# Cross-attention with layernorm on one core: masks turned into biases by ScalarE, and another order of all engines

## The chip, the cores and the metric

The kernel runs on one core of one Trainium2 chip. The metric is device time in microseconds (us), the median of several runs. Before the change it is 514.48 us (three runs: 514.18, 514.48, 514.49).

The core has five instruction streams that run side by side and meet at semaphores: TensorE (PE, with its weight loads as PEld), VectorE (DVE), ScalarE (ACT), GpSimd (POOL) and SyncE (SP, which here only issues DMAs). Each stream executes strictly in the order in which its instructions stand.

## The reference

Queries come from `x` (4 batches of 2048 rows, 512 wide), keys and values from a context of 77 rows per batch; 16 heads of 32. A mask hides keys. The residual `x` is added and each row is layer-normalised with a gain and a shift.

```python
qs  = (q @ wq).reshape(Bq, Lq, H, HD).transpose(0, 2, 1, 3)
ks_ = (k @ wk).reshape(Bq, Lk, H, HD).transpose(0, 2, 1, 3)
vs  = (v @ wv).reshape(Bq, Lk, H, HD).transpose(0, 2, 1, 3)
scores = jnp.einsum('bhqd,bhkd->bhqk', qs, ks_) / jnp.sqrt(jnp.float32(HD))
scores = jnp.where(mask[:, None, :, :], -jnp.inf, scores)
attn_w = jax.nn.softmax(scores, axis=-1)
attn = jnp.einsum('bhqk,bhkd->bhqd', attn_w, vs)
attn = attn.transpose(0, 2, 1, 3).reshape(Bq, Lq, H * HD)
out = attn @ wo + q
mu = jnp.mean(out, axis=-1, keepdims=True)
var = jnp.mean((out - mu) ** 2, axis=-1, keepdims=True)
return (out - mu) / jnp.sqrt(var + EPS) * gamma + beta
```

The mask reaches the kernel as bytes, 96 per row (the last 19 of the 77 keys stand twice, for the two layouts of even and odd heads).

## The kernel before

The 8192 rows are 64 tiles of 128 rows, `t`. Two tiles are a block `b`, four a group `g` for the query projection, 16 a batch. The projections run in split single precision: an operand is a rounded part and a rest, and each product is three matmuls.

The work of a tile, by the letters that the kernel's order uses:

- `Q`: one quarter of a group's query projection, 12 matmuls of 512 columns; `q`: DVE copies it out of PSUM.
- `S t`: the scores of a tile on PE, into four PSUM banks, one for each head position. `T t.j`: DVE reads bank j, adds the mask's bias and takes the row maxima, four heads at a time. `e t.j`: ACT's exponentials, each with a read of its accumulator. `r`: DVE's reciprocal of the sums, `n`: POOL's product with it, `t`: DVE's transpose, `P`: DMAs that regroup the transposed weights.
- `V b`: the product with the values for a block, into two banks; `a` (ACT) and `b` (DVE) take the rounded part and the rest out of them. `O t`: the output projection, 12 matmuls. `+` or `&`: DVE adds the residual; `s`: DVE's moments; `v`, `k`, `f`, `)`: POOL's rsqrt, ACT's scale, POOL's gain and shift; `x` and `w` load and store rows. The last eight tiles take their end on DVE (`u`, `y`, `z`) and their residual rows from an `X` or `&`.
- `g`, `i`, `j`: the load of two of the four column chunks of a group's transposed `x`, its rounding on ACT and its rest on POOL.
- `L`: the load of a batch's mask, `M t.n`: DVE turns the bytes of n tiles into a bfloat16 bias (byte times -3.38e38). `= t.n`: the same on ACT.
- Before the steady state: `A`, `C`, `R`, `p` load the value and output weights, `F` and `G` take their rests on DVE (lines 355 and 367: two operands in SBUF), `B` projects the values, `D` takes them out, `Z` places them.

The order of all engines is written out by hand: the string `ORDER` holds some 2150 words, and each engine's instructions are issued in the order of its words. `SLOTS` says which buffer each allocation takes; the entry "mm" names one of the eight PSUM banks at each use. A PE step therefore waits for the words that empty its banks (`T`, `q`, `b`, `+`), for its operands, and for nothing else. Three buffers `pbuf` hold the score tiles in turn, and one buffer holds the mask bytes.

Of the kernel before, what the change touches and what calls it, by code (L numbers as in the profile page):

```python
# [33 lines left out]
for b in range(4):  # L34
# [19 lines left out]
e4.0 e4.3 r4 e6.3 e6.1 e6.0 q10 D1 P1.0s P1.4s Q8 q8 P1.5s T6.2 e6.2 P1.6s Q9 q9 P1.11s P1.9s P1.8s S5 T5.3 e5.3 T5.0
e5.0 n4 t4 S7 r6 T7.2 e7.2 T5.1 T7.3 e7.3 T7.1 P1.3s P1.10s T7.0 P1.7s e7.1 Z4.s Z5.s x2 g9 Q11 Q14 x3 T5.2 x0 q11 q14
n6 t6 e7.0 r7 Q13 q13 n7 S9 T9.0 T9.1 T9.2 e5.1 Z14.s Z16.s e5.2 r5 V1 a1.0 b1.0 t7 P3.5s e9.1 a1.1 b1.1 P3.3s P3.10s
V0 a0.0 T9.3 b0.0 P3.7s n5 P3.2s t5 P2.6s P3.8s P3.0s P3.9s a0.1 P3.1s i8 j8 i9 e9.0 e9.2 P3.11s N P3.6s O2 b0.1 +2 s2
P2.11s P3.4s Y0 P2.8s S8 T8.0 j9 O3 +3 T8.1 T8.2 s3 v1 O0 T8.3 S10 T10.3 T10.1 T10.2 P2.2s e9.3 r9 n9 e8.0 e8.1 e8.2
e8.3 r8 n8 +0 O1 +1 s1 P2.1s P2.5s t9 T10.0 k2 e10.1 P2.3s k3 f3 )3 P2.7s P2.0s e10.2 t8 Q15 e10.0 V3 a3.0 b3.0 S11
T11.2 a3.1 e10.3 T11.0 P2.9s r10 P2.10s P2.4s e11.2 g10 P4.7s P4.2s w3 s0 v0 Z7.s T11.1 e11.1 x4 P4.9s e11.0 Q12 q15  # L60
P4.4s q12 T11.3 b3.1 Q18 q18 S12 T12.3 P4.1s T12.0 M28.4 e11.3 r11 P4.5s x7 Z15.s V2 k1 T12.1 S13 n10 t10 e12.3 T12.2
n11 f2 t11 P4.10s g11 P4.6s e12.0 T13.1 T13.2 M16.4 P4.3s P4.11s T13.3 a2.0 P5.6s P4.0s e12.2 M20.4 P4.8s Z11.s P5.7s
x6 e12.1 a2.1 r12 n12 e13.2 O7 +7 P5.2s x5 P5.9s P5.4s i10 j10 T13.0 P5.11s )2 w2 b2.0 s7 P5.0s O6 Q17 q17 e13.1 S14
T14.1 T14.2 T14.0 e13.3 e13.0 k0 i11 e14.1 t12 r13 e14.2 T14.3 e14.3 Q19 q19 P5.8s Q16 +6 s6 b2.1 M24.4 f1 n13 S15
T15.2 t13 T15.1 V4 a4.0 P5.10s v3 k6 T15.0 f0 )0 )1 Z13.s Z12.s P5.1s x8 P5.5s g12 b4.0 q16 P6.5s w0 L2 e14.0 e15.0
j11 T15.3 a4.1 b4.1 f6 P5.3s O5 +5 O4 +4 S16 T16.3 T16.0 P6.9s r14 w1 n14 s5 T16.2 T16.1 P6.4s t14 P6.1s k7 f7 g13
e15.2 e15.3 e16.3 e15.1 r15 S17 T17.1 T17.3 T17.0 )6 n15 s4 v2 e16.2 Q21 q21 Q20 i12 )7 e16.1 O9 x9 T17.2 P6.10s P6.8s
e17.1 e17.0 i13 e16.0 j13 P6.0s P6.6s Z8.s P6.3s t15 +9 S18 T18.0 P6.2s T18.1 T18.2 T18.3 r16 n16 q20 V5 a5.1 O8 +8 s9
P6.7s P6.11s a5.0 e17.3 j12 e17.2 b5.1 P7.0s P7.7s r17 n17 Q23 s8 q23 V6 P7.6s e18.3 e18.0 e18.2 P7.8s x11 P7.3s g14
P7.2s P7.11s Z6.s t16 v4 e18.1 S19 T19.0 T19.3 e19.3 w7 P7.1s P7.5s T19.2 P7.9s r18 b5.0 P7.4s w6 t17 P8.4s n18 P7.10s  # L70
a6.0 g15 k4 e19.0 k9 f9 a6.1 P8.9s Q22 P8.3s P8.8s T19.1 q22 O11 +11 )9 i14 b6.0 b6.1 j14 e19.1 Q25 q25 S20 T20.0
T20.1 T20.3 x13 k8 k5 e19.2 P8.11s e20.3 x10 P8.1s g16 f4 )4 w4 t18 S21 T21.3 r19 w9 T21.1 f8 n19 P8.6s P8.2s f5 Q26
s11 q26 e20.0 T21.2 e21.2 e20.1 T20.2 e20.2 O13 +13 O10 P8.0s t19 P8.5s T21.0 r20 n20 +10 s10 S22 T22.1 T22.3 e21.1
i15 j15 P8.10s V7 a7.1 b7.1 e21.0 x12 P8.7s Q24 T22.2 P9.11s P9.7s a7.0 P9.3s )5 e21.3 e22.1 e22.3 s13 t20 Z9.s Z10.s
P9.10s P9.4s v5 k10 T22.0 e22.0 r21 n21 P9.0s O12 +12 b7.0 q24 s12 v6 k11 f10 f11 Q27 q27 S23 T23.1 T23.0 T23.2 V8 g17
)10 P9.8s P9.2s x16 w5 P9.5s x15 P9.9s e22.2 r22 t21 e23.0 k13 P9.1s n22 )8 S24 T24.1 T24.2 O15 +15 a8.0 b8.0 T24.0
T24.3 P9.6s a8.1 T23.3 P10.0s P10.7s O14 Q29 t22 e23.1 i16 e23.3 S25 b8.1 P10.10s P10.8s x14 T25.1 T25.0 w10 x17 w8
e23.2 e24.0 +14 q29 e24.2 s14 e24.3 j16 f13 )13 g18 i17 V9 a9.1 r23 n23 T25.2 T25.3 e25.0 e24.1 s15 v7 a9.0 k12 )11
j17 e25.1 e25.2 e25.3 O16 +16 s16 t23 r24 O17 P10.9s +17 S26 P10.5s P10.11s x18 P10.4s s17 T26.2 v8 b9.0 n24 P10.3s
P10.6s P10.1s T26.3 T26.0 b9.1 r25 n25 k17 P10.2s Q31 q31 P11.3s w13 P11.0s P11.7s g19 P11.1s P11.5s T26.1 Q30 q30 t24  # L80
Q28 q28 e26.2 S27 T27.3 T27.1 k16 e26.1 P11.8s f16 )16 x19 P11.9s T27.0 P11.11s P11.6s P11.10s P11.4s V10 t25 P12.10s
k14 f14 e27.1 S28 T28.1 T28.2 P11.2s a10.0 b10.0 T28.3 w11 P12.7s a10.1 f17 )17 w17 P12.8s P12.6s P12.3s e26.3 P12.11s
e26.0 r26 n26 k15 e27.3 f15 T27.2 e27.2 T28.0 e28.0 b10.1 i18 P12.0s x21 x20 Q33 q33 O19 P12.5s +19 t26 e27.0 e28.1
e28.2 s19 P12.2s O18 +18 S29 T29.1 T29.3 )14 V11 a11.1 f12 j18 e29.3 T29.2 e29.2 r27 n27 s18 T29.0 t27 w16 g21 P12.4s
S30 T30.1 b11.1 T30.3 O20 i19 v9 )15 P12.1s T30.2 +20 e28.3 r28 T30.0 s20 j19 k18 f18 a11.0 Q35 q35 Q32 w15 q32 b11.0
e29.0 P13.3s P13.6s e30.0 w14 P12.9s g20 x23 x22 P13.4s P13.2s n28 )18 P13.1s P13.5s P13.0s P13.7s e29.1 O21 +21 s21
M36.4 v10 M32.4 r29 n29 t28 Q37 S31 T31.0 T31.3 q37 P13.11s e30.2 w18 P13.8s e30.1 e30.3 k19 P13.10s V12 a12.0 f19
P13.9s )19 )12 w12 t29 P14.11s r30 e31.3 Q34 q34 a12.1 k21 f21 k20 f20 P14.0s P14.6s e31.0 T31.1 e31.1 T31.2 e31.2 i21
b12.1 O22 +22 S32 T32.0 T32.1 T32.2 e32.0 b12.0 i20 e32.1 T32.3 e32.3 O23 +23 s23 n30 t30 P14.10s Q38 q38 r31 j21 S33
T33.1 T33.0 V13 a13.0 b13.0 e32.2 P14.4s P14.7s P14.9s x25 x24 P14.5s P14.2s )21 n31 P14.1s P14.8s x27 P14.3s T33.2  # L90
e33.2 M44.4 S34 s22 r32 T33.3 )20 w20 e33.3 t31 a13.1 T34.0 T34.2 g23 M40.4 b13.1 O24 O25 w19 +24 P15.8s e33.0 e33.1
r33 w21 n32 x26 P15.2s L3 P15.4s v11 k22 k23 f22 n33 e34.2 t32 +25 T34.1 f23 )23 j20 Q39 q39 T34.3 e34.3 Q36 s24 q36
S35 T35.0 T35.1 T35.2 T35.3 e34.1 e34.0 P15.10s P15.0s t33 x28 P15.9s V14 a14.0 P15.1s a14.1 e35.0 r34 n34 i23 e35.2
# [5 lines left out]
Q40 q40 S39 T39.2 T39.0 T39.1 i25 j25 e39.0 f26 P17.11s V16 a16.1 r38 n38 t37 T39.3 S40 b16.1 T40.1 e39.3 a16.0 b16.0
T40.2 P17.4s w27 e39.1 w24 P17.3s O30 O31 P17.9s +30 T40.0 e40.1 P18.7s T40.3 t38 e39.2 x32 e40.0 v14 k28 )25 V17  # L100
a17.0 r39 n39 g24 i24 j24 S41 T41.0 T41.1 s30 f28 P18.10s O32 Q44 P18.11s k29 f29 T41.3 e41.3 )29 a17.1 t39 T41.2 Q45
b17.1 +32 x31 +31 s31 e40.3 e40.2 P18.9s b17.0 P18.0s r40 P18.4s P18.1s P18.5s P18.3s P18.8s e41.2 x33 e41.0 e41.1 v15
S42 s32 T42.1 P19.0s P19.8s P19.4s P19.10s )28 T42.2 T42.3 n40 P18.6s r41 n41 )26 P19.7s P18.2s O33 +33 q45 q44 w25
# [671 lines left out]
```

## Time and profile before

One execution was profiled: 514.09 us, of which 512.3 us are the span from the first to the last instruction.

| engine | busy us | share of the span |
|---|---|---|
| PE | 500.2 | 98% |
| DVE | 471.6 | 92% |
| ACT | 464.1 | 91% |
| POOL | 422.8 | 83% |

The last matmul starts at 504.98 us; the rest of the span is the end of the last tiles on DVE and their stores. The granted TensorE clock was 0.998. A share of busy time does not say who waits for whom; rows of single instructions do, and these carry the argument below. In such a row stand the start and the duration in us, the engine, the line, the operation, output and inputs, shapes, a count, and in brackets the engine's idle time before it with what ended it.

### The profile page before, as it was taken

The page shows a single profiled execution, that of the slowest core. Times are in us where ns is not written, and L with a number is a line of the kernel's source. Part 1 is how long each engine was busy: PE and PEld are TensorE (multiplying, and loading weights), DVE is VectorE, ACT ScalarE, POOL GpSimd, SP SyncE. Part 2 cuts the span into 40 slices and gives each one's busy share as a digit, 9 for nine tenths or more (in the row PEclk, how much of TensorE's full clock was granted, in tenths as well). Part 3 has the DMA queues.
Part 4 walks back from the last instruction along what each step waited for, and adds up shares of the span by engine and source line. Part 5 has one row for each costly group of instructions (what it writes and reads, how often), then busy time and mean ns, then how long its engine had stood idle before and what let it go on. Part 6 is the DMA issues. An engine that isn't in the chain of part 4 may idle for free. (4 is left out here: it accounts for less than half of the span.)

```text
span 512.3 us, 20317 instructions
## 1 busy us (share of the span) xinstructions
PE 500.2 (98%) x6833; PEld 384.4 (75%) x6833; DVE 471.6 (92%) x2562; ACT 464.1 (91%) x2223; POOL 422.8 (83%) x387
## 2 busy tenths in 40 slices
PE   9999999999999999999999999999999999999994
PEld 6986777787778778777777878768777777777763
DVE  5799999999999989988999999897999999999997
ACT  6699999999998999999989999899999999999530
POOL 2476456678989898999978899979899989998995
PEclk9999999999999999999999999999999999999999
DMA  8946668878788778878787888766897587979565
GB/s 301 398 146 191 168 172 201 233 210 220 184 224 254 192 206 247 216 206 238 207 236 194 215 242 203 213 216 195 214 244 194 146 263 216 244 214 224 162 199 207
DMA packets 59325, 110.85 MB, mean 216 GB/s; under 512 B 9494, under 2 KB 11822, under 8 KB 59222
## 3 DMA queue, kind: packets, MB, share of 16 engines
q1 hardware_dynamic: 55766, 102.75, 71.9%
q0 software_dynamic: 2496, 5.77, 3.9%
q10 hardware_dynamic: 960, 1.05, 0.8%
q8 instruction: 54, 0.88, 0.8%
q14 instruction: 49, 0.40, 0.2%
HBM read 41.79 MB, written 16.78 MB: 114 GB/s over the span
## 5 line engine op out<-in xcount | busy, mean ns | idle before, releaser
L434 ACT ACTIVATE pbuf<-pbuf,nm 128x77 f32<-128x77 f32 x1024 | 353.0, 355 | 11.2 <-DVE nm L419 11.0
L434 ACT ACTIVATION_READ_ACCUMULATOR pbuf<-pbuf,nm 128x1 f32 x1024 | 200.0, 195 | 0.0
L419 DVE CUSTOM_DVE_ANT_0 pbuf<-sc,mb 128x77 f32<-128x77 f32 x1024 | 170.6, 232 | 7.5 <-PE sc L402 5.8
L449 POOL TENSOR_TENSOR pbuf<-pbuf,ri 128x1232 f32<-128x1232 f32 x63 | 142.9, 2272 | 33.4 <-DVE ri L444 29.1
L551 PE MATMUL po<-woh,AH 128*128 128x512 f32 x256 | 103.7, 405 | 2.0 <-DVE nm L419 1.5
L275 PE MATMUL pq<-xth,wqh 128*128 128x512 f32 (+1 forms) x256 | 100.0, 391 | 0.3
L551 PE MATMUL po<-woh,AL 128*128 128x512 f32 x256 | 100.0, 391 | 0.0
L551 PE MATMUL po<-wol,AH 128*128 128x512 f32 x256 | 99.9, 390 | 0.0
L470 DVE STREAM_TRANSPOSE B<-pbuf 128x1280 f32<-128x1280 f32 x64 | 96.0, 1501 | 4.0 <-POOL pbuf L449 2.2
L275 PE MATMUL pq<-xtl,wqh 128*128 128x512 f32 (+1 forms) x256 | 98.1, 383 | 0.0
L275 PE MATMUL pq<-xth,wql 128*128 128x512 f32 (+1 forms) x256 | 98.0, 383 | 0.0
L419 DVE DVE_READ_ACCUMULATOR2_ANT nm<- 128x1 f32 x1024 | 84.5, 83 | 0.0
L269 POOL TENSOR_TENSOR xtl<-xtf,xth 128x1024 fp32r<-128x1024 f32 x28 | 68.2, 2435 | 10.4 <-ACT xth L265 9.8
L592 POOL TENSOR_TENSOR o<-o,gam 128x512 f32<-128x512 f32 x56 | 72.3, 1296 | 3.8 <-ACT o L589 3.8
L595 POOL TENSOR_TENSOR o<-o,bet 128x512 f32<-128x512 f32 x56 | 72.1, 1293 | 1.8
L402 PEld LDWEIGHTS sc<-kct,q 32*64 32x64 f32 x4096 | 52.0, 130 | 23.5 <-issue 11.7
L402 PE MATMUL sc<-kct,q 32*64 32x77 f32 x4096 | 61.7, 238 | 1.7 <-DVE q L289 1.1
L551 PEld LDWEIGHTS po<-woh,AH 128*128 128x128 f32 x256 | 48.0, 188 | 17.8 <-ACT pbuf L434 1.6
L495 PE MATMUL pa<-PT,vsb 96*32 96x256 f32 x992 | 59.8, 382 | 0.0
L275 PEld LDWEIGHTS pq<-xth,wqh 128*128 128x128 f32 x256 | 48.1, 188 | 12.6 <-issue 1.0
L551 PEld LDWEIGHTS po<-woh,AL 128*128 128x128 f32 x256 | 48.0, 188 | 11.0 <-DVE AL L528 0.6
L275 PEld LDWEIGHTS pq<-xth,wql 128*128 128x128 f32 x256 | 48.1, 188 | 9.5
(95 smaller groups left out, 642.8 us busy)
## 6 DMA issues: line engine op xcount, KB each, us to landing
PT<-B SPq DMA_DIRECT2D x343, 128.0 KB
xtf<-xT SPq DMA_DIRECT2D x28, 512.0 KB
o<-x SPq DMA_DIRECT2D x56, 256.0 KB
out<-o SPq DMA_DIRECT2D x56, 256.0 KB
PT<-B POOLq DMA_DIRECT2D x25, 128.0 KB, 5.0
xtf<-xT SPq DMA_DIRECT2D x4, 256.0 KB
stage_a<-wq SPq DMA_DIRECT2D x4, 256.0 KB
stage_a<-wk SPq DMA_DIRECT2D x4, 256.0 KB
```

Source lines behind the costliest of these rows:

```text
L269: nc.gpsimd.tensor_tensor(l[:, c : c + 2], fx.pop((g, c)), xh[g][:, c : c + 2].bitcast(F32), ALU.subtract)
L275: nc.tensor.matmul(pq, w[:, c, m * P : (m + 1) * P], r[g][:, c, rs], start=(n == 0), stop=(n == 11))
L402: mm = nc.tensor.matmul(sc[j][r0 : r0 + SR, g * NK : (g + 1) * NK], qs[q, g, rs.start + r0 : rs.start + r0 + SR], kct[q, g, t // TPB, keys ...
L419: nc.vector.tensor_tensor_reduce(pb[:, h // 2, (h % 2) * NK : (h % 2 + 1) * NK], scs[t][j][:, g * NK : (g + 1) * NK], mb[:, t % TPB, keys_ ...
L434: nc.scalar.activation(pb[:, h // 2, (h % 2) * NK : (h % 2 + 1) * NK], pb[:, h // 2, (h % 2) * NK : (h % 2 + 1) * NK], AF.Exp, bias=nmax[t ...
L449: nc.gpsimd.tensor_tensor(pv, pv, rv.to_broadcast((P, NP, 2, NK)), ALU.mult)
L470: nc.vector.transpose(bt.rearrange("p c q r -> p q c r"), pbuf[t % NPB].rearrange("p q (c r) -> p q c r", c=5),)
L495: nc.tensor.matmul(pas[b, g // 2][HD * j : HD * (j + 1), (g % 2) * BLK : (g % 2 + 1) * BLK], vsb[:, 2 * b // TPB, h % 2, HD * (h // 2) : H ...
L551: nc.tensor.matmul(pos[t], a[:, c, rs], w[:, c, :], start=(first and c == 0 and n == 0), stop=(c == NC_D - 1 and n == 2),)
L592: nc.gpsimd.tensor_tensor(od[t], od[t], gam, ALU.mult)
L595: nc.gpsimd.tensor_tensor(od[t], od[t], bet, ALU.add)
```

## The change

Only `ORDER` and `SLOTS` differ. The first 60 words, up to the first query visit after the scores of tile 3, are the same. After that:

- The twelve words `M16.4` to `M60.4` (DVE, 128x384 each: the masks of batches 1 to 3) are gone, and six words `=16.8`, `=24.8`, `=32.8`, `=40.8`, `=48.8`, `=56.8` (ACT, 128x768 each) stand in the string. The masks of batch 0 stay with DVE, at the same early place. `=16.8` follows the load `L1` of its mask directly in the string; the others follow theirs at a distance.
- All other words are the same ones in another order, on every engine.

```diff
@@ ORDER @@
-T0.2 H0 T0.0 j3 e0.0 T1.0 T0.3 e0.2 T1.1 Q4 T1.2 e0.3 F0 T1.3 I0 e1.2 r0 n0 S2 q4 e1.0 S3 T2.3 T2.0 Q7 i5 T2.1 e1.3 F2
+T0.2 H0 T0.0 j3 e0.0 T1.0 T0.3 e0.2 T1.1 Q4 T1.2 e0.3 F0 T1.3 I0 e1.2 r0 n0 S2 q4 e1.0 S3 T2.3 T2.0 Q7 N Y0 x1 Q5 i5
...
+e9.2 L1 =16.8 Z15.s b0.0 x3 x4 Z5.s i9 j9 a0.1 P3.2s t5 O2 S8 +2 e9.0 T8.1 e8.1 T8.2 e8.2 b0.1 T8.0 e8.0 O3 P3.0s +3
...
@@ SLOTS @@
-    "xtf": "010101010101101010101010110110",
+    "xtf": "010101010101010100010101101001",
...
```

Three places, as the built programs have them. A name such as `sc_43_1_5928` is the bank of tile 43's scores for head position 1, `mb_3` and `m8_3` are bias and bytes of batch 3's mask; the last number of a name only tells allocations apart.

First, DVE at the scores of tile 43. Before, a mask of batch 3 stood between two banks of that tile:

```order
L419 ISA pbuf1_81,nm_43_5963<-sc_43_1_5928,mb_2_4288 128x77
L419 ISA nm_43_5963 128x1
L385 TENSOR_SCALAR mb_3_6044<-m8_3_4788 128x384
L419 ISA pbuf1_81,nm_43_5963<-sc_43_3_5930,mb_2_4288 128x77
L419 ISA nm_43_5963 128x1
```

Now there is no mask on DVE from tile 16 on. That mask's bytes are read by ACT, between a scale of tile 34 and the exponentials of tile 45:

```order
L434 ACTIVATE pbuf0_80,sum_45_6203<-pbuf0_80,nm_45_6198 128x77 x4
L524 CAST AH_19_6357<-pa_19_1_6340 128x512
L589 ACTIVATE o_34_6117<-o_34_6117,rn_17_6259 128x512
L383 ACTIVATE mb_3_6360<-m8_3_6031 128x768
L434 ACTIVATE pbuf0_80,sum_45_6203<-pbuf0_80,nm_45_6198 128x77 x4
```

What moved is one conversion of 384 elements from DVE to ACT, joined there with the next 384.

Second, DVE ahead of the scores of tile 4, which read the query copies of group 1 (`q_1`). Before:

```order
L470 STREAM_TRANSPOSE B_0_633<-pbuf1_81 128x8x5x32
L289 COPY q_1_552<-pq_1_3_603 128x512
L289 COPY q_1_552<-pq_1_2_639 128x512
L289 COPY q_1_552<-pq_1_1_673 128x512
L419 ISA pbuf1_81,nm_4_780<-sc_4_1_745,mb_0_292 128x77
```

Now (the last bank of tile 3, then the copies; two more `L367` stand a few rows higher, between the transpose and that bank):

```order
L419 ISA nm_3_665 128x1
L367 TENSOR_TENSOR wol_73<-stage_b_84,woh_72 128x512
L289 COPY q_1_552<-pq_1_3_603 128x512
L289 COPY q_1_552<-pq_1_1_623 128x512
L444 RECIPROCAL ri_2_756<-sum_2_670 128x16
L335 COPY v_0_778<-pv_0_765 128x512
L419 ISA pbuf1_81,nm_4_822<-sc_4_1_787,mb_0_292 128x77
```

Three splits of the output weights now stand between that transpose and the last copy, where before one stood ahead of the transpose; and PE now runs two value projections (`B1`, `B0`) ahead of these scores where before it ran one (`B0`).

Third, DVE at the end, around the value product of block 30 (`AL_30`), which the output projection of tile 61 reads. Before:

```order
L563 TENSOR_TENSOR po_59_8815<-po_59_8815,xth_14_7812 128x512
L603 BN_STATS st_59_8871<-po_59_8815 128x6
L605 BN_AGGR mvt_59_8873<-st_59_8871 128x2
L563 TENSOR_TENSOR po_58_8883<-po_58_8883,xth_14_7812 128x512
L603 BN_STATS st_58_8897<-po_58_8883 128x6
L605 BN_AGGR mvt_58_8899<-st_58_8897 128x2
L528 TENSOR_TENSOR AL_30_8921<-pa_30_0_8901,AH_30_8919 128x512
L628 SCALAR_TENSOR_TENSOR po_59_8815<-po_59_8815,mvt_59_8873,gam_76 128x512
L628 SCALAR_TENSOR_TENSOR po_57_8709<-po_57_8709,mvt_57_8868,gam_76 128x512
L528 TENSOR_TENSOR AL_30_8921<-pa_30_1_8902,AH_30_8919 128x512
```

Now:

```order
L470 STREAM_TRANSPOSE B_31_8767<-pbuf0_80 128x8x5x32
L563 TENSOR_TENSOR po_59_8846<-po_59_8846,xth_14_8144 128x512
L603 BN_STATS st_59_8860<-po_59_8846 128x6
L605 BN_AGGR mvt_59_8862<-st_59_8860 128x2
L563 TENSOR_TENSOR po_56_8771<-po_56_8771,xth_14_8144 128x512
L603 BN_STATS st_56_8866<-po_56_8771 128x6
L605 BN_AGGR mvt_56_8868<-st_56_8866 128x2
L563 TENSOR_TENSOR po_58_8871<-po_58_8871,xth_14_8144 128x512
L603 BN_STATS st_58_8885<-po_58_8871 128x6
L605 BN_AGGR mvt_58_8887<-st_58_8885 128x2
L528 TENSOR_TENSOR AL_30_8909<-pa_30_0_8889,AH_30_8907 128x512
L528 TENSOR_TENSOR AL_30_8909<-pa_30_1_8890,AH_30_8907 128x512
```

The moments of tile 57 went ahead of the last transpose, and the two ends of tiles 59 and 57 behind both rests of block 30.

More of the change, by code (lines that the diff above doesn't have):

```diff
@@ L54 @@
[L54 to L93, printed above, removed]
@@ L99 @@
[L99 to L103, printed above, removed]
@@ new lines @@
+e38.0 e37.2 P17.6s e37.3 r37 t36 f25 n37 )24 f26 P17.4s Q41 q41 w12 Q42 q42 S39 T39.2 T39.3 T39.0 t37 T39.1 e38.3
+e38.2 e38.1 w22 P17.8s r38 e39.3 )25 )26 n38 g24 V16 a16.1 b16.1 P17.9s w27 x32 P17.10s x31 e39.0 P18.6s P18.9s w25
+P18.2s x30 P18.5s P18.7s s29 v14 e39.1 a16.0 S40 T40.1 T40.2 T40.3 b16.0 t38 Q45 e39.2 r39 n39 e40.1 i24 e40.2 O31 +31
+T40.0 q45 O30 w24 P18.8s P18.10s j24 s31 S41 T41.2 x33 P18.1s T41.3 T41.1 T41.0 +30 P18.11s s30 v15 e40.3 k29 V17
+e40.0 k28 i25 e41.0 r40 n40 j25 t39 O32 a17.1 b17.1 Q47 S42 +32 s32 T42.2 T42.0 q47 e41.1 e41.2 e41.3 r41 e42.2 k31
@@ new lines @@
+P24.2s e52.2 b22.0 P24.4s P24.8s x47 T52.0 O43 e52.3 P24.5s O45 r51 S53 +43 s42 s43 v21 t50 P24.1s T53.2 e52.0 +45
+e52.1 V23 a23.1 Q58 T53.1 P24.7s w40 P24.6s x44 P24.11s b23.1 e53.2 a23.0 T53.3 e53.3 )41 P24.0s P24.3s r52 b23.0
+T53.0 P24.10s n51 P24.9s t51 P25.1s P25.9s P25.5s P25.4s S54 T54.0 k42 k43 e53.0 e53.1 T54.1 q58 T54.2 s45 r53 Q57 q57
+n52 t52 O44 +44 s44 f42 )42 w41 i30 e54.0 T54.3 e54.2 S55 T55.2 P25.0s V24 =56.8 a24.0 x49 f43 )43 P25.7s P25.2s
+P25.6s P25.11s w43 n53 T55.3 e54.3 v22 k44 t53 T55.1 b24.0 P26.2s P26.3s j30 P25.3g P25.8s P25.10s a24.1 e55.2 b24.1
```

144 lines of the change are left out of this document (89 added, 55 removed).

## The prediction

> **What bounds the kernel now.** I read the page's busy times first, then the stretches, then every place where PE starts late.
>
> ```profile
> PE 500.2 (98%) x6833; PEld 384.4 (75%) x6833; DVE 471.6 (92%) x2562; ACT 464.1 (91%) x2223; POOL 422.8 (83%) x387
> 60.00:120.00 60.00, 59.62 (x912) 45.32 (x912) 58.19 (x356) 59.88 (x306) 38.36 (x33) 1.00 0.75 197
> 120.00:180.00 60.00, 59.94 (x864) 46.12 (x864) 55.52 (x328) 58.31 (x284) 52.87 (x44) 1.00 0.82 219
> 300.00:360.00 60.00, 58.55 (x769) 44.74 (x768) 53.66 (x302) 57.12 (x275) 55.81 (x47) 1.00 0.75 207
> 360.00:420.00 60.00, 60.00 (x840) 45.82 (x833) 58.15 (x334) 59.59 (x287) 54.49 (x53) 1.00 0.79 208
> ```
>
> The columns after a stretch are its length and the busy time of PE, PEld, DVE, ACT and POOL. From 60 us on PE is hardly ever idle, and the change takes no matmul from it. So only what PE loses between its steps can be won: places where a step starts later than the one before it allows. ACT comes close behind: it idles 0.12 us between 60 and 120 and 0.41 between 360 and 420, but 1.69 and 2.88 in the other two stretches. DVE has 1.8 to 6.3 us free in each. PE is thus bound by its own work, with two engines so near that a short delay shows.
>
> The undisturbed pace comes from these rows: 12 matmuls of 512 columns take 2.81 us up to the scores behind them (39.10 to 41.91), and the scores of a tile 0.88 (265.87 to 266.75).
>
> ```profile
> 39.10 0.39 PE L326 MATMUL pv<-wvh,ctx_h 128*128 128x512 f32 x1
> 41.91 0.51 PE L402 MATMUL sc<-kct,q 32*64 32x77 f32 x16
> 43.25 0.82 PE L402 MATMUL sc<-kct,q 32*64 32x77 f32 x48 [0.82 <-DVE q L289]
> 43.99 0.43 PE L326 MATMUL pv<-wvh,ctx_h 128*52 128x512 f32 x1
> ...
> 60.72 0.90 PE L402 MATMUL sc<-kct,q 32*64 32x77 f32 x58 [0.26 <-DVE q L289]
> 61.55 0.50 PE L275 MATMUL pq<-xth,wqh 128*128 128x512 f32 x1
> ...
> 265.87 0.95 PE L402 MATMUL sc<-kct,q 32*64 32x77 f32 x64
> 266.75 1.93 PE L495 MATMUL pa<-PT,vsb 96*32 96x256 f32 x32
> 268.62 0.42 PE L402 MATMUL sc<-kct,q 32*64 32x77 f32 x6
> 269.35 0.89 PE L402 MATMUL sc<-kct,q 32*64 32x77 f32 x58 [0.32 <-DVE nm L419]
> 270.18 0.50 PE L551 MATMUL po<-woh,AH 128*128 128x512 f32 x1
> ```
>
> The scores of tile 4 take 2.08 us instead of 0.88: 1.2 lost, waiting for DVE's query copies. Those of tile 36 take 1.56 (268.62 to 270.18): 0.68 lost, waiting for DVE's maxima. The scores of tile 7 still have 58 of their 64 matmuls to do at 60.72, where a wait for DVE ends; the next step follows at 61.55, and about 1.0 is lost. Every large loss ends with DVE emptying a PSUM bank or writing an operand.
>
> **The change: the masks leave DVE.** The largest loss has a mask in it.
>
> ```profile
> 330.85 2.38 POOL L269 TENSOR_TENSOR xtl<-xtf,xth 128x1024 fp32r<-128x1024 f32 x1
> 331.20 2.24 DVE L385 TENSOR_SCALAR mb<-m 128x384 bf16<-128x384 uint8 x1
> 331.72 0.95 PE L402 MATMUL sc<-kct,q 32*64 32x77 f32 x64
> 333.37 0.23 DVE L419 CUSTOM_DVE_ANT_0 pbuf<-sc,mb 128x77 f32<-128x77 f32 x1
> 334.00 0.23 DVE L419 CUSTOM_DVE_ANT_0 pbuf<-sc,mb 128x77 f32<-128x77 f32 x1
> 334.13 0.50 PE L551 MATMUL po<-woh,AH 128*128 128x512 f32 x1 [1.45 <-DVE nm L419]
> ...
> L385 DVE TENSOR_SCALAR mb<-m x17: 206/354/2243, 16.3 to 439.0; 128x384 bf16<-128x384 uint8 x15, 128x96 bf16<-128x96 uint8 x1, 128x288 bf16<-128x288 uint8 x1
> ```
>
> The mask takes 2.24 us against a median of 0.354 (minimum, median and maximum stand in the last row). It starts while a POOL product is running and ends 0.21 us behind it (331.20 + 2.24 = 333.44; 330.85 + 2.38 = 333.23): it seems to stand still until POOL is done. Behind it in DVE's order are the maxima of tile 43's bank 3, whose bank the output projection of tile 34 takes; PE waits 1.45 us. Without the mask the four maxima start at 331.28 instead of 333.37, and end 2.09 earlier than at 334.0: the whole wait goes. **Minus 1.45.** At worst another DVE delay takes its place, so the bounds are -1.45 and 0. The other eleven masks are worth nothing to PE directly: DVE's free 1.8 us and more per stretch cover 0.35 each.
>
> **The change: ACT gets them.** No row shows this form on ACT. Casts of 512 and 1024 elements between SBUF tiles bracket it:
>
> ```profile
> L247 ACT CAST woh<-stage_a 128x512 fp32r<-128x512 f32 x4 | 2.5, 620 | 1.2 <-DMA stage_a<-wk 1.2
> L265 ACT CAST xth<-xtf 128x1024 fp32r<-128x1024 f32 x28 | 29.2, 1047 | 0.0
> ...
> 249.41 1.07 ACT L265 CAST xth<-xtf 128x1024 fp32r<-128x1024 f32 x1
> 250.35 0.39 ACT L434 ACTIVATE pbuf<-pbuf,nm 128x77 f32<-128x77 f32 x1
> ```
>
> 768 elements lie midway: 0.83 us, and as the next operation starts some 0.1 before the end (249.41 + 1.07 against 250.35), ACT is held for 0.74. Six of them are 4.4 us. Queued behind each are exponentials, and behind those the reciprocal on DVE, which waits in order with the bank releases that PE needs.
>
> ```profile
> DVE ri L444 <- ACT pbuf L434: 2.9, 6, 0.9
> ```
>
> Before, DVE stood still for ACT at six reciprocals, 2.9 us in all and 0.9 at most: ACT's lateness does reach DVE, seldom. The bounds are 0 and 4.4. The first two masks fall between 60 and 120 us, where ACT has 0.12 us to spare, so of their 1.48 something must be handed on, against DVE's 1.81 free there; the other four meet 1.7 to 2.9 us of idle time in most stretches. I take about a quarter of the first two, nearer to the lower end: **plus 0.4**.
>
> [...]
>
> **The change: scores of tile 4.** DVE and PE are set against each other from the same start.
>
> ```profile
> 36.62 2.11 DVE L367 TENSOR_TENSOR wol<-stage_b,woh 128x512 fp32r<-128x512 f32 x1
> ...
> 35.60 2.58 POOL L449 TENSOR_TENSOR pbuf<-pbuf,ri 128x1232 f32<-128x1232 f32 x1 [0.79 <-DVE ri L444]
> 38.15 2.85 POOL L269 TENSOR_TENSOR xtl<-xtf,xth 128x1024 fp32r<-128x1024 f32 x1
> 44.91 2.41 POOL L269 TENSOR_TENSOR xtl<-xtf,xth 128x1024 fp32r<-128x1024 f32 x1 [3.91 <-ACT xth L265]
> ...
> L248 DVE TENSOR_TENSOR wql<-stage_a,wqh 128x512 fp32r<-128x512 f32 x4 | 2.8, 689 | 1.4 <-ACT wqh L247 1.4
> ```
>
> The output weights' splits (L367) are held up by POOL too: the first ends 0.55 behind a POOL product (36.62 + 2.11 = 38.73; 38.18), where an equal split with POOL at rest takes 0.69. PE now does one visit more before these scores, so it arrives 2.81 later. DVE does three splits instead of one and four more maxima (0.63, the time from 333.37 to 334.00). If all three splits fall into POOL's idle 3.9 us (41.0 to 44.9), DVE adds 0.63 + 3 x 0.6 - 2.03 = 0.4; if each takes the 2.03 of the first, 0.63 + 2 x 2.03 = 4.7. The loss of 1.2 becomes 1.2 - 2.81 + 0.4 to 4.7: none, or up to 3.1. The first two splits look free of POOL and the third not, which gives about 1.8 for DVE and nearly no loss; since the splits of the value weights before them also move up against a POOL product, I take 0.8: **minus 0.4**, with bounds -1.2 and +1.9. The scores of tile 7 wait for the same copies and the same DVE work: no change.
>
> **The change: the end.**
>
> ```profile
> 490.13 1.13 PE L540 MATMUL po<-xtl,ident 128*128 128x512 f32 x2
> 491.71 0.50 PE L551 MATMUL po<-woh,AH 128*128 128x512 f32 x1 [0.46 <-DVE AL L528]
> ...
> 484.14 1.51 DVE L470 STREAM_TRANSPOSE B<-pbuf 128x1280 f32<-128x1280 f32 x1
> 487.11 0.67 DVE L603 BATCH_NORM_STATS2 st<-po 128x6 f32<-128x512 f32 x1
> 487.91 0.67 DVE L563 TENSOR_TENSOR po<-po,xth 128x512 f32<-128x512 f32 x1
> 491.00 0.66 DVE L528 TENSOR_TENSOR AL<-pa,AH 128x512 fp32r<-128x512 f32 x1
> ```
>
> Tile 61's projection waits for block 30's rest, which stands last in a DVE queue that runs without a gap from the transpose at 484.14. The moments of tile 57 (487.11 to 487.91, 0.8) are now ahead of that transpose, so the rest can start at 490.2. **Minus 0.8**; bounds -0.8 and 0, if the transpose comes later by as much. From there PE's work is the same, and what follows the last matmul also.
>
> **The change: everything else.** Between tiles 8 and 57 the same words stand in another order. Losses such as tile 36's 0.68 belong to one order and vanish with it, and others of their size can come. I take 0, with -1.7 (tile 36's and tile 7's both gone) and +1.7 (as much again) as bounds.
>
> **The sum** against the profiled execution: 514.09 - 1.45 + 0.4 - 0.4 - 0.8 = 511.84 us. The median of the runs shown is 0.39 above that execution, so the forecast is 512.2.
>
> **The rivals.**
>
> *More is won.* DVE, rid of twelve masks, is ahead everywhere, and the losses of tiles 4, 7 and 36 go entirely: 514.48 - 1.45 - 0.8 - 1.2 - 1.0 - 0.68 = 509.4; with ACT's 0.4 and one of the small ones left, 510.4. For it speaks that every loss named ended on DVE; against it that PE's order was packed as closely to DVE before, and that a new order has its own pinches.
>
> *The early stretch takes the gain.* All three splits meet POOL, and tile 4's scores lose 3.1: 514.48 - 1.45 - 0.8 + 1.9 + 0.4 = 514.5, no change. POOL was busy for 21.6 of the 30 us from 30 on:
>
> ```profile
> 30.00:60.00 30.00, 28.98 (x363) 22.48 (x354) 28.99 (x152) 28.13 (x146) 21.56 (x9) 1.00 0.57 160
> ```
>
> *ACT sets the pace* (the other side). Each mask delays the exponentials behind it, the reciprocals and transposes follow on DVE, and the bank releases queued behind these reach PE late. It is slower than before once 3.3 us of the 4.4 come through (1.45 + 0.8 + 1.03 of measurable difference), that is with five of the six: 514.48 - 2.25 + 3.7 = 515.9, and with all six 516.7. For it speak the two nearly full stretches; against it the free time in the others, and that DVE waited for ACT only 2.9 us.
>
> *The first mask is late.* Its load now stands right ahead of it in the string; should ACT reach it first, it would stand still in order. SP has only its own issues to go through and can run ahead, so I give this little; a wait of 3 us would cost about what it lasts, 515.
>
> **How the numbers follow.** Forecast 0.45, with a range of its own from 511.0 to 513.5; more is won 0.15; early stretch 0.20; ACT 0.17; late mask 0.03. This kernel can be told from no change at about 0.2%, 1.03 us: faster is below 513.45, slower above 515.5. Nine tenths of the forecast, all of the second case and a tenth of the third are faster: 0.58. Slower are most of ACT's and the late mask's cases and a little of the early one: 0.19. The rest, 0.23, is no change. The range from 510.3 to 516.0 leaves out the better half of the second case and the worse half of ACT's.
>
> **What would show it.** In the new trace no DVE operation at line 385 after 20 us, and six at line 383 on ACT of 0.80 to 0.87 us; no PE wait above 0.5 us at the scores of tile 44 and the projection behind them; block 30's first rest at about 490.2 less what was won before it; ACT's busy time in the four stretches shown up by 0.74 for each mask that falls into it, and DVE's waits at the reciprocal still below 5 us. The prediction is wrong if PE's losses before 62 us grow by over 1 us, if reciprocals wait for ACT for 6 us or more, or if the masks on ACT take over 1.1 us.

## The result: slower by 1%, and the profile after

| | median us | lowest to highest | runs |
|---|---|---|---|
| before, beside it | 514.49 | 514.18 to 515.38 | 4 |
| changed | 520.40 | 516.32 to 523.75 | 4 |

The ratio is 1.0106, with an interval of 1.0074 to 1.0138: slower. A second set of ten runs of the same kernel gave 518.55 (1.0062, 1.0035 to 1.0089). The forecast was 512.2, its range ended at 516.0. The times scatter far more than those of before (7.4 us against 1.2); the last section comes back to it.

The profiled execution of the changed kernel took 516.32 us (span 514.4), 2.23 more than that of before. From its page, the busy times:

```profile
PE 500.5 (97%) x6833; PEld 384.3 (75%) x6833; DVE 466.5 (91%) x2550; ACT 468.9 (91%) x2229; POOL 421.7 (82%) x387
```

PE's busy time is what it was (500.2). Two places hold what it lost. The first is the scores of tile 4. From the timeline, PE, DVE and POOL (start, duration, then the idle time before in brackets):

```profile
44.61 0.39 PE L402 MATMUL sc<-kct,q 32*64 32x77 f32 x16
48.09 0.68 PE L402 MATMUL sc<-kct,q 32*64 32x77 f32 x37 [3.08 <-DVE q L289]
...
31.81 3.59 DVE L355 TENSOR_TENSOR wvlAL<-stage_b,wvh 128x512 fp32r<-128x512 f32 x2
42.24 1.29 DVE L367 TENSOR_TENSOR wol<-stage_b,woh 128x512 fp32r<-128x512 f32 x2
44.08 2.75 DVE L367 TENSOR_TENSOR wol<-stage_b,woh 128x512 fp32r<-128x512 f32 x1
46.76 1.27 DVE L289 COPY q<-pq 128x512 f32<-128x512 f32 x2
...
32.03 2.82 POOL L269 TENSOR_TENSOR xtl<-xtf,xth 128x1024 fp32r<-128x1024 f32 x1
43.92 2.36 POOL L269 TENSOR_TENSOR xtl<-xtf,xth 128x1024 fp32r<-128x1024 f32 x1 [2.40 <-ACT xth L265]
```

PE does 16 of the 64 matmuls and then stands for 3.08 us for a query copy (this view ends at 48.5 us, so it counts 37 of the other 48). The copies start at 46.76, behind the third split of the output weights, which took 2.75 us where the two before it took 1.29 together. It ends at 46.83, 0.55 behind the POOL product (43.92 + 2.36 = 46.28). The last split of the value weights does the same eleven us earlier: 31.81 + 3.59 = 35.40, again 0.55 behind POOL's 34.85. DVE runs on between the two with no pause above 0.2 us.

The second place is the value product of block 27 (line 495):

```profile
456.75 0.95 PE L402 MATMUL sc<-kct,q 32*64 32x77 f32 x64
457.63 0.63 PE L495 MATMUL pa<-PT,vsb 96*32 96x256 f32 x7
459.88 1.70 PE L495 MATMUL pa<-PT,vsb 96*32 96x256 f32 x25 [1.61 <-issue]
```

PE stops in the middle of the product, after seven of 32 matmuls; "issue" means that the profile shows nothing that it waited for. From its first matmul to the next step (461.51) the block takes 3.88 us instead of 1.86.

What the change was to win did come. Scores and projection that were 1.45 us apart now follow each other, here for tiles 44 and 45 in one row:

```profile
333.81 1.75 PE L402 MATMUL sc<-kct,q 32*64 32x77 f32 x128
335.71 0.47 PE L551 MATMUL po<-woh,AH 128*128 128x512 f32 x1
...
L383 ACT ACTIVATE mb<-m 128x768 bf16<-128x768 uint8 x6 | 5.1, 843 | 0.0
L385 DVE TENSOR_SCALAR mb<-m 128x384 bf16<-128x384 uint8 (+2 forms) x5 | 1.2, 314 | 0.0
```

From the starts of PE's steps in both traces, what each loses beyond its usual length: tile 4's scores 3.34 instead of 1.20 (+2.1), block 27's product 2.0 instead of nothing; tiles 44, 36 and 7 together 0.4 instead of 3.2 (-2.8). Small losses elsewhere in the scores add 0.7, so the scores as a whole come out even, and the profiled execution is later by what block 27 lost.

### The profile page after: what moved, and what is told of

Same layout as the page of the kernel before. It is cut to its first block, busy times and chain, and to the rows that moved or that the text cites. A ratio compares the mean times of both kernels' runs of the same rounds, so it can differ in the third digit from the quotient of the medians.

```text
span 514.4 us, 20304 instructions
## 1 busy us (share of the span) xinstructions
PE 500.5 (97%) x6833; PEld 384.3 (75%) x6833; DVE 466.5 (91%) x2550; ACT 468.9 (91%) x2229; POOL 421.7 (82%) x387
## 4 chain that ended last, share of the span: by engine, by line
PE 71%; DVE 17%; ACT 4%; DMA 3%; SPq 2%; issue 2%; POOL 1%; ACTq 0%; DVEq 0%
PE pq L275 27%; PE po L551 23%; PE sc L402 8%; PE pa L495 8%; DVE B L470 4%; DVE pbuf L419 4%; DMA PT<-B 3%; ACT pbuf L434 3%; PE pk L298 1%; PE pq L669 1%; DVE AL L528 1%; SPq L481 1%; DVE po L628 1%; DVE st L574 1%; PE pw L642 1%
```

## Experiments

Three explanations of the loss were on trial: the splits that meet POOL ahead of tile 4 (S), the masks on ScalarE (M), and a wait of PE for its own instructions at block 27 (F). All times are medians, ratios are against runs of the kernel before on the same chip.

### The changed kernel again

No edit; a second trace of it, and a reference for the next three.

> The changed kernel once more, unaltered. What is to be explained: its one trace shows TensorE idle for 3.1 us in the scores of tile 4, and its executions lay between 516.3 and 523.8 us with mean granted clocks of 0.996 down to 0.984. Theory S (splits): the wait in the scores of tile 4, behind two weight splits that DVE can't start while a GpSimd product runs, costs 2 to 3 us by itself and sometimes lets the granted clock fall to half for several us. It expects the wait of 3 to 3.5 us at 45 us in any trace, 516 to 524 us, and in an execution of over 518 us a stretch at half clock that begins between 46 and 54 us. Rival M (masks on ScalarE): the six masks hold ScalarE up and the spread comes from there; a slow trace would show ScalarE late by several us after 80 us and a full clock. Rival F (instruction fetch): TensorE starves for instructions, as at 458 us in the first trace (2.0 us); a slow trace would show several such waits with no releaser.

Measured: 518.55 us (515.52 to 520.9). Tile 4's scores wait 3.10 us again, and block 27's product stops at the same matmul, 1.6 us longer than usual. Both losses belong to the order, not to one execution. This time the clock was also granted at half from 48.02 to 51.44 us, right behind the wait, where S had put it.

### Both splits moved

```diff
- ... F1 e1.1 F3 R2 F2 T2.1 T2.2 j5 ...
+ ... F1 e1.1 F3 R2 T2.1 T2.2 F2 j5 ...
- ... G0 T3.0 G2 q7 e3.0 q5 B1 ...
+ ... G0 T3.0 q7 e3.0 q5 G2 B1 ...
```

> The changed kernel with two words moved on DVE, nothing else: the third split of the output weights (G2) behind the last query copy of group 1, and the last split of the value weights (F2) behind the maxima of tile 2. Theory S: the wait in the scores of tile 4 falls from 3.3 us to under 1, the profiled time is 513 to 514, the executions agree within 1 us, and the granted clock is 0.996 to 0.998 in all of them. Rival M: no change, 516 to 524. Rival F: the wait at 45 us goes but the spread stays, with some executions above 518.

Measured: 512.84 us, ratio 0.9966 (0.9948 to 0.9984): faster than before, 5.7 us less than the changed kernel. Scores of tile 4, and the third output split with its POOL product:

```profile
45.19 0.95 PE L402 MATMUL sc<-kct,q 32*64 32x77 f32 x64
...
43.40 1.29 DVE L289 COPY q<-pq 128x512 f32<-128x512 f32 x2
44.60 2.33 DVE L367 TENSOR_TENSOR wol<-stage_b,woh 128x512 fp32r<-128x512 f32 x1
...
44.00 2.38 POOL L269 TENSOR_TENSOR xtl<-xtf,xth 128x1024 fp32r<-128x1024 f32 x1 [3.15 <-ACT xth L265]
```

The split still stands still for POOL and still ends 0.55 behind it (46.93 against 46.38), but the copies are ahead of it and PE waits for nothing. S holds for the wait. It missed the spread: the runs still lie 3.7 us apart and not within 1 us, and block 27's stop (1.6 us) is still there. Two words in the order were worth more than the whole loss. The wait is 3.1 us and the gain 5.7; the rest is taken up in the last section.

### Only the output split moved

```diff
- ... G0 T3.0 G2 q7 e3.0 q5 B1 ...
+ ... G0 T3.0 q7 e3.0 q5 G2 B1 ...
```

> The changed order with only the third split of the output weights moved behind the last query copy; the split of the value weights that meets the other POOL product stays. DVE runs without a pause from 31 to 48 us, so both should count: of the 3.1 us at tile 4's scores 2.7 go and about 0.4 to 0.6 stays there or at the steps before, 512.8 to 513.8 in all. If only the last split counts, there is nothing left at tile 4 and the time is that with both moved, 512.84. If the splits are not the cause, the wait stays at 3 us and the time at 518.

Measured: 512.98 us, 0.9968 (0.9952 to 0.9984), which cannot be told from both moved. A rest of 0.42 us stays at tile 4:

```profile
45.89 0.82 PE L402 MATMUL sc<-kct,q 32*64 32x77 f32 x48 [0.42 <-DVE q L289]
```

So moving the third output split takes away 2.7 of the 3.1 us, as long as it held DVE. That is not a division of blame: the value split still made DVE 2.2 us late here, which PE no longer felt but for 0.42. What moving the value split alone would give was not run.

### The masks back on DVE

The changed order, each of the six ScalarE masks written as two on DVE at the same place in the string:

```diff
- ... =32.8 ...
+ ... M32.4 M36.4 ...
```

> The changed kernel's order with the six ScalarE masks given back to DVE, two masks of four tiles at the place of each. Theory S: as the changed kernel, 516 to 524, with the wait of 3 to 3.5 us at tile 4 and the spread, plus 0 to 2 us where a DVE mask is held up by a GpSimd product. Rival M: 513 to 515 and no spread. Rival F: spread stays.

Measured: 526.03 us, 1.0223 (1.0169 to 1.0276), 7.5 slower than with ScalarE. The first pair, the POOL product beside it, and the projection that follows (line numbers are one higher here):

```profile
80.39 2.76 DVE L386 TENSOR_SCALAR mb<-m 128x384 bf16<-128x384 uint8 x2
83.07 0.68 DVE L529 TENSOR_TENSOR AL<-pa,AH 128x512 fp32r<-128x512 f32 x1
...
80.46 4.93 POOL L270 TENSOR_TENSOR xtl<-xtf,xth 128x1024 fp32r<-128x1024 f32 x2
...
83.81 0.50 PE L552 MATMUL po<-woh,AH 128*128 128x512 f32 x1 [2.22 <-DVE AL L529]
```

This is what the prediction read at tile 44: a DVE mask held by POOL, the rest of a value product behind it, and PE waiting. M falls for this order; here the masks are better on ScalarE. How much better the comparison doesn't say, since the order was made without DVE masks in it. Nor are the 7.5 us all waits for masks: in the profiled execution, the slowest of the four, block 27's stop lasted 2.98 us and four windows of 3.41 us ran at half clock (last section).

### The masks alone, in the old order

The order of before, with the six ScalarE masks where DVE's first masks of a pair stood:

```diff
- ... T12.0 M28.4 e11.3 ... T13.2 M16.4 P4.3s ... e12.2 M20.4 P4.8s ... b2.1 M24.4 f1 ...
+ ... T12.0 =24.8 e11.3 ... T13.2 =16.8 P4.3s ... e12.2 P4.8s ... b2.1 f1 ...
- ... q46 T43.1 M48.4 x35 T43.3 ...
+ ... q46 T43.1 =48.8 x35 T43.3 ...
```

> The kernel before, in its own order, with the twelve DVE masks of batches 1 to 3 replaced by six ScalarE masks of eight tiles, each at the place of the earlier of its two. The prediction's terms for the masks alone: minus 1.45 us at the scores of tile 44, plus 0 to 1 for ScalarE: 513.0 to 514.0. Theory S and rival F: 512.9 to 514. Rival M: 516 or more.

Measured: 514.85 us, 1.0003 (0.9988 to 1.0017): no change, and not the 513.0 to 514.0 of the prediction's terms. The 1.5 us at tile 44 are gone, and as much is lost elsewhere: tile 17's scores lose 1.24 instead of 0.27, tile 34's 0.51, tile 36's 0.84 instead of 0.68. Tile 17, on ACT, DVE and PE:

```profile
125.85 0.59 ACT L524 CAST AH<-pa 128x512 fp32r<-128x512 f32 x1
...
126.47 0.69 DVE L528 TENSOR_TENSOR AL<-pa,AH 128x512 fp32r<-128x512 f32 x1 [1.49 <-ACT AH L524]
127.08 1.28 DVE L560 TENSOR_TENSOR o<-po,o 128x512 f32<-128x512 f32 x2
...
128.41 0.90 PE L402 MATMUL sc<-kct,q 32*64 32x77 f32 x58 [0.26 <-DVE o L560]
```

ACT is two masks behind when it rounds a value product; DVE stands still for it (1.49 instead of 0.46 before), and queued behind that stand the two residual sums that empty the banks for the scores.

### Only the later masks

As above, with the masks of batch 1 back on DVE; four ScalarE masks are left.

```diff
- ... T12.0 =24.8 e11.3 ... T13.2 =16.8 P4.3s ... e12.2 P4.8s ... b2.1 f1 ...
+ ... T12.0 M28.4 e11.3 ... T13.2 M16.4 P4.3s ... e12.2 M20.4 P4.8s ... b2.1 M24.4 f1 ...
```

> The order of before with the masks of batches 2 and 3 alone on ScalarE (four operations of 128x768 in the places of eight), those of batch 1 left on DVE. If the step that had masks on ScalarE come through to PE only where ScalarE has no time to spare (60 to 120 us) is right, tile 17's scores lose 0.3 again instead of 1.24, tile 44's 1.5 are gone, 0.4 to 0.8 comes back at tiles 34 and 36, and the time is 513.2 to 513.8. If it makes no difference where a mask stands, the gain is eaten again by four masks: 514.4 to 515.

Measured: 513.28 us, 0.9977 (0.9968 to 0.9986): 1.2 faster than before. Tiles 16 and 17 run as before the change (0.27 lost at tile 17), and tile 44's scores and the projection behind them also:

```profile
126.26 1.76 PE L402 MATMUL sc<-kct,q 32*64 32x77 f32 x128
...
332.55 0.95 PE L402 MATMUL sc<-kct,q 32*64 32x77 f32 x64
333.43 0.50 PE L551 MATMUL po<-woh,AH 128*128 128x512 f32 x1
```

Tile 34's scores lose 0.50, as with six masks. So in the old order the two early masks, where ACT has nothing to spare, cost PE 1.6 us (514.85 against 513.28), and the four later ones at most that 0.5.

### The stop at block 27: 16 PE instructions more

The kernel with both splits moved, and the nine warm-up matmuls of 512 columns written as seventeen of 271. The columns are the same in number; 16 instructions more (eight weight loads, eight matmuls) stand ahead of everything on PE.

```diff
-WARM = 9
+WARM = 17
-        nc.tensor.matmul(pw, warm[:, :P], warm, start=True, stop=True)
+        nc.tensor.matmul(pw[:, :271], warm[:, :P], warm[:, :271], start=True, stop=True)
```

> The changed order with its two splits moved, and the nine warm-up matmuls of 512 columns written as seventeen of 271: the same columns, but 16 more instructions (a weight load and a matmul each) stand ahead of all other work on PE. Theory F, the stop in block 27's value product is a wait for PE's own next 256 instructions, which came 1.6 us late because two short steps stand back to back just there: with 16 instructions more the boundary falls elsewhere, block 27's product takes 1.86 to 2.0 us instead of 3.48, and the median falls from 512.84 by 1.2 to 1.7, to about 511.3. A rival, the stop belongs to block 27 itself (its operands, its banks): it stays at about 3.4 us there, and the time stays at 512.6 to 513.0. If long waits of PE make the clock drop, the spread of the runs also narrows, from 3.7 us to about 2.

Measured: 510.99 us (510.44 to 512.29), 0.9932 (0.9916 to 0.9948), 1.85 less than without these instructions, and the fastest of all: 3.5 us below before. Block 27 runs through:

```profile
455.61 1.93 PE L495 MATMUL pa<-PT,vsb 96*32 96x256 f32 x32
457.47 0.50 PE L551 MATMUL po<-woh,AH 128*128 128x512 f32 x1
```

The same edit in the kernel before, where nothing stopped:

> The kernel before, with only its nine warm-up matmuls of 512 columns written as seventeen of 271, 16 PE instructions more. Its shortest stretch between a request for instructions and their need grows from 4.9 to 6.1 us, and no stop was there before: no change, 514.2 to 514.9. If the finer warm-up itself were worth the 1.85 us that the changed order gained by it, this would be 512.6.

Measured: 514.97 us, 1.0001 (0.999 to 1.0012). The finer warm-up by itself is worth nothing.

### Provoking the stop in the kernel before

Only the warm-up differs from before: 104 PE instructions more, about the same columns.

```diff
-WARM = 9
+WARM = 61
-        nc.tensor.matmul(pw, warm[:, :P], warm, start=True, stop=True)
+        nc.tensor.matmul(pw[:32, :76], warm[:, :32], warm[:, :76], start=True, stop=True)
```

> The kernel before, with only its nine warm-up matmuls of 512 columns written as sixty-one of 76 columns (32 weights each): about the same columns, 104 PE instructions more, all ahead of the first projection. By theory F, a boundary of 256 instructions now falls behind a pair of short steps at four places, near 210, 254, 300 and 391 us, where only 3.3 us lie between the request and the need; PE stops there with no engine to wait for, 0.3 to 2 us each: two to four stops, 1.5 to 5 us in all, 516 to 519.5. By the rival, in which the stop belongs to block 27's product, nothing stops at these places and the time is that of before, 514.2 to 515.

Measured: 522.08 us (521.26 to 525.4), 1.0155 (1.0127 to 1.0183). All four stops are there, and no others like them. Their rows, with the row ahead of the first:

```profile
210.24 0.87 PE L402 MATMUL sc<-kct,q 32*64 32x77 f32 x55
213.21 0.41 PE L402 MATMUL sc<-kct,q 32*64 32x77 f32 x9 [2.10 <-issue]
...
260.15 0.36 PE L402 MATMUL sc<-kct,q 32*64 32x77 f32 x7 [0.58 <-issue]
...
306.11 0.35 PE L402 MATMUL sc<-kct,q 32*64 32x77 f32 x4 [1.14 <-issue]
...
398.30 0.50 PE L551 MATMUL po<-woh,AH 128*128 128x512 f32 x1 [1.03 <-ACT pbuf L434]
```

The profile puts the fourth down to ACT. It is counted here because of where it stands and because of its packet of instructions (last section).

Counting PE's instructions (weight loads, matmuls, semaphore waits and drains) up to each such stop, in the traces of six kernels, every one above 0.75 us:

```
kernel                    stop at us    PE instructions before it       time to the next, us
changed                   457.88        12993 = 50 x 256 + 193          1.99
changed, again            459.51        12993 = 50 x 256 + 193          1.58
both splits moved         454.73        12993 = 50 x 256 + 193          1.59
output split moved        455.53        12993 = 50 x 256 + 193          1.88
masks back on DVE         466.93        12993 = 50 x 256 + 193          2.98
before, 104 more          210.89         6081 = 23 x 256 + 193          2.32
before, 104 more          259.34         7361 = 28 x 256 + 193          0.81
before, 104 more          304.75         8641 = 33 x 256 + 193          1.36
before, 104 more          397.05        11201 = 43 x 256 + 193          1.25
changed, 16 more          246.07         6849 = 26 x 256 + 193          1.23
changed, again            245.77         6849 = 26 x 256 + 193          0.79
```

All eleven fall on the same count within 256, whichever step stands there; of the other waits of PE that are this long none does. F holds: what stops is the instruction stream. That a PE step waits for its banks and operands "and for nothing else", as the description of the kernel had it, leaves this out. The times came out above the 519.5 that F allowed; the four stops are within its 5 us (5.7 less four ordinary gaps of 0.2), and 1.5 of the rest were lost in one window at half clock (last section).

### The wait at tile 4 alone

The changed order with the seventeen warm-up matmuls, so that the stop at block 27 is gone and the splits are where the change put them.

> The changed order with its splits where the change put them, and the warm-up as seventeen matmuls of 271 columns, so that the stop at block 27 is gone and the long wait at tile 4's scores alone is left. Against the kernel with both splits moved as well (510.99): the wait itself adds about 3.1 us, 514.1. If a wait of this length also lowers the granted clock, every run in which most of it falls into one 3.4 us window of the clock shows half clock in the window behind it and 1.7 us more: runs at about 514.1 and at 515.8, a median between them, and mean clocks lower by 0.003 in the later ones. If the clock has nothing to do with it, all runs lie within 1 us of 514.1.

Measured: 516.59 us (514.45 to 519.39), 1.0032 (1.0015 to 1.0049). Against the changed order without the edit (518.55) that is 2.0 less, against both edits (510.99) 5.6 more. The two corrections add up: 2.0 and 5.7 each alone, 7.6 together. The median is above both values that were expected, 514.1 and 515.8. The wait is 3.09 us as before; what lies behind it is new:

```profile
44.71 0.39 PE L402 MATMUL sc<-kct,q 32*64 32x77 f32 x16
48.19 0.82 PE L402 MATMUL sc<-kct,q 32*64 32x77 f32 x48 [3.09 <-DVE q L289]
...
247.31 0.49 PE L402 MATMUL sc<-kct,q 32*64 32x77 f32 x21 [1.01 <-issue]
```

The last row is a stop of the kind above, at tile 32. The changed order had it in its second trace too (0.79 us, in the table), so the 16 instructions did not bring it alone.

## Why the prediction was wrong

**What bounds the kernel** was read rightly: PE's losses between steps decided the time, in every run.

**Masks leave DVE, -1.45: right.** The wait at tile 44 is gone in the changed order and wherever DVE's mask left that place; putting masks back beside POOL brought a wait of the same kind (2.22). One reading was incomplete: of the eleven masks "worth nothing" another had met POOL, at 255.01 us, and took 1.45 and not 0.35; PE lost nothing by it.

**ACT gets them, +0.4: about 0 for PE in this order, and wrong in its test.** A mask took 0.84 us, as bracketed. But DVE's waits for ACT at the reciprocal grew from 2.9 to 9.5 us, beyond the 6 that I had set as the mark of failure:

```profile
DVE ri L444 <- ACT pbuf L434: 9.5, 16, 1.2
```

ACT's busy time did not rise by two masks between 60 and 120 us either (59.55 us after 59.88), since other work of its had moved. PE lost nothing by it that can be seen: in the profiled execution there is no wait above 0.5 us between tiles 7 and 57 but block 27's. So in this order the 9.5 us at reciprocals were no cost, by my reading because nothing that PE needs at once stood behind them. In the old order ACT's lateness was a cost, though not at a reciprocal: at tile 17 it came through the rounding that DVE's rest waits for, and the two early masks gave back the 1.45 (1.6 by the medians, 1.0 of it at tile 17). The rival in which ACT sets the pace was thus right about the mechanism and wrong about this order. The late-mask rival did not come up: the first mask ran at 79.21 us, 0.85 long, with nothing waiting.

**Scores of tile 4, -0.4: the step that failed.** What it mis-sized is DVE's splits beside POOL. It read "the first two splits look free of POOL and the third not, which gives about 1.8 for DVE and nearly no loss". The first two were free (1.29 together) and the third met POOL, as said; but it held DVE for 2.68 us (44.08 to 46.76) and not 2.03: it began 0.16 us behind the start of POOL's product, which took 2.36, and ended 0.55 behind its end. The value split ahead lost 2.2 in a queue that has no pause to absorb it; the step had named it and allowed it some 0.6 (2.4 for DVE in all, 1.8 of them the output splits and maxima). PE could go on 4.8 us later than before (48.09 against 43.25), which is the far end of what I had worked out for DVE (4.7) and not its lower part: 2.2 for the value split, 1.85 for the output splits, 0.63 for the four more maxima, 0.16 for a small pause. PE lost 3.34 there: +2.1, just beyond the upper bound of +1.9. The prediction's own sign of being wrong, losses before 62 us that grow by over 1 us, came. The early-stretch rival had this loss to 0.2 us, with a chance of 0.20, but by luck: all three output splits were to meet POOL, and one did; the rest was the value split's.

**The end, -0.8: came to about -0.3.** DVE and PE at block 30's rest:

```profile
486.98 1.48 DVE L470 STREAM_TRANSPOSE B<-pbuf 128x1280 f32<-128x1280 f32 x1
...
493.00 1.25 DVE L528 TENSOR_TENSOR AL<-pa,AH 128x512 fp32r<-128x512 f32 x2
...
493.72 0.50 PE L551 MATMUL po<-woh,AH 128*128 128x512 f32 x1 [0.16 <-DVE AL L528]
```

The projection waits 0.16 instead of 0.46. The transpose was to start no later than before. It came at 486.98, 0.5 later when PE's own delay of 2.3 is taken off, so 0.3 of the 0.8 was left; the bad bound of the step named this.

**Everything else, 0: failed by what it did not contain.** The scores of tile 36 became free and those of tile 7 lose 0.4 instead of 1.0, a gain of 1.3 together (for tile 7 I had forecast none). Against it stand small losses of 0.7 and the stop at block 27, 2.0, which no step of mine and no rival had, since the trace of before has no such wait. With the terms as measured, -1.5 + 0 + 2.1 - 0.3 - 1.3 + 0.7 + 2.0 = +1.7 of the 2.2 us by which the profiled execution grew.

**From the profiled execution to the median** I added 0.39. It was 516.32 and the median 520.40. Behind tile 4's wait the clock fell to half in the second trace of the changed kernel (48.02 to 51.44 us), and in the profiled execution it did not: its mean clock was 0.996, those of the other three 0.984 to 0.990. Where in these three the clock fell was not profiled.

Without these two places the changed order is what it was forecast to be, and a little more: 510.99 where the likeliest case said 512.2, and the case in which more is won, 510.4. Part of that is not the forecast's doing: with the splits moved the 1.2 us that the kernel before lost at tile 4 are gone too.

## What to carry to other kernels

Cost a split of DVE on two SBUF tiles by what POOL does at that moment: here one that began just after a POOL product of 2.36 us took 2.75 us, where two undisturbed ones took 1.29 together, and what was queued behind it was late by as much. In a kernel where PE hardly rests, try such work behind what PE waits for; two places in the order were worth 5.6 us here (518.55 to 512.98). And after any reordering look for stops with no engine behind them, and count PE's instructions up to them: here all eleven stood at 193 within 256. 16 instructions more at the start moved the stop at block 27 away (1.85 us), and 104 more made four stops in the kernel before.

## What the runs showed of the hardware

**The instruction stream can stop PE.** The pages of the kernel before and of the changed one list the same row, a DMA queue for instructions:

```profile
q8 instruction: 54, 0.88, 0.8%
```

54 packets of 0.88 MB are 16 KB each, and 13 955 recorded PE instructions (13 666 of them loads and matmuls) over 54 are 258: about 256 instructions a packet. In the changed kernel the packet that block 27 needed was on its way from 457.09 for 1.31 us, and was there at 458.40, 0.5 us after PE had run out at 457.88; PE went on at 459.88. At all eleven stops, the one put down to ACT among them, PE went on 1.3 to 1.5 us after its packet was there. So PE stopped even where its packet landed a little ahead of its need, as five of the eleven did, by 0.1 to 0.6 us. Before, the packet of the same number started at 453.87 and took 2.65 us, and was there 1.0 us ahead of its need; PE went on 1.3 us after it and lost at most 0.3.

The packets start with a varying delay: in the changed trace 0.1 to 5.6 us, median 2.1, behind the earliest point in the count at which any of them started (297 instructions ahead of the need). At the four places provoked above, where scores and a value product stand back to back and PE goes through 192 instructions in 2.7 us, the stretch from that point to the need is 3.4 us; the shortest in the kernel before is 4.9. Block 27 is another case: there the stretch is 5.1 us in the changed kernel and 4.9 before, and the difference is the packet, which started 4.3 us behind that point against 1.3. In all five traces of the new order without more instructions it was 3.8 to 5.2 us, in three of the old order 1.3 to 2.7. What delays a packet, these runs do not show. At the eleven places PE went without an instruction for 0.8 to 3.0 us.

**A wait can cost more than its length, by the clock.** The stretches behind a long stop, in windows of 3.41 us: that is how long half clock lasted in the records (48.02 to 51.44 us in the second trace of the changed kernel, 48.87 to 52.28 in the first fence below), and they are laid from the places where the clock changed. The columns are the window, its length, busy time of PE, PEld, DVE, ACT and POOL, the granted clock, DMA share and GB/s. First the changed kernel with 16 instructions more, then the profiled execution of the changed one:

```profile
42.05:45.46 3.41, 3.05 (x29) 2.15 (x27) 3.41 (x17) 3.41 (x16) 1.43 (x1) 1.00 0.67 156
45.46:48.87 3.41, 0.68 (x48) 0.66 (x48) 3.38 (x5) 2.61 (x16) 1.43 (x2) 1.00 0.90 227
48.87:52.28 3.41, 3.41 (x20) 1.67 (x9) 2.69 (x26) 2.93 (x17) 2.79 (x2) 0.50 0.51 173
```

```profile
43.12:46.53 3.41, 1.88 (x23) 1.18 (x22) 3.41 (x10) 3.41 (x18) 2.36 (x1) 1.00 0.87 203
46.53:49.95 3.42, 1.86 (x53) 1.33 (x54) 3.25 (x18) 2.13 (x14) 1.68 (x1) 1.00 0.75 222
```

The same wait, 3.1 us. Where one window held most of it, PE ran the next window at half clock and lost another 1.5 us (the visit of 12 matmuls behind the wait took 4.44 us instead of 2.91); where it fell across two, nothing followed. The same happened behind the 2.32 us stop of the kernel before with 104 more instructions: PE was busy for 1.31 us of the window from 210.00 to 213.41, and the next had clock 0.50. In the traces of these kernels' main part, seven windows with PE busy for 0.7 to 1.9 us were followed by half clock, and those with 2.05 and more were not, with one exception: in the kernel with its masks back on DVE the half clock behind the 2.98 us stop lasted two windows, though PE was busy for all of the first. Between 1.56 and 1.91 there are both: 1.86 and 1.88 above without, 1.91 in another kernel with, and 1.56 at the very end of the kernel before without. So where the boundary lies stays open. Since the windows fall differently in each execution (those above begin at 42.05 and at 43.12 us), the time becomes a matter of luck: the changed kernel's four runs go from 516.32 at a mean clock of 0.996 to 523.75 at 0.984. Half clock for 2 x 0.012 x 520 = 12.5 us, three to four windows, would by this estimate cost 6.2 of these 7.4 us; where those windows lay is not on record. With the wait alone left the median is 2.5 above the 514.1 that its length gives (1.0 of it the stop at tile 32, in the one execution that was profiled); with neither stop left, six runs lie within 1.9 us. PE had not rested for a whole window there: it was still busy for 0.68 us in the one above and for 1.31 us in that from 210.00, with waits of 3.09 and 2.32 us, shorter than the window.

**DVE and POOL.** In all thirteen cases in three traces (six of before, three of the changed kernel, four of that with both splits moved) a split of 512 elements that began during a POOL product ended 0.55 us behind it, whether it had begun 0.2 or 2.6 us after its start; two undisturbed ones took 1.29 together. Four that began 0.1 to 0.2 us ahead of a product took 0.62 to 0.78 us and were not held; the product took 2.58 to 2.88 us instead of 2.25 to 2.42. A mask, which reads one tensor, was held as well (2.24 us before, 2.51 with the masks back on DVE, ending 0.2 behind POOL). So meeting a POOL product held DVE for the rest of the product and 0.55 us with a split, and for the rest of it and 0.2 with a mask. Through what the two engines hold each other up, these runs do not show.
